# Graph network layer: another order for layernorm's products, and a running-max step or one-hot piece after each max of banks

## The chip, the cores and the metric

The kernel runs on one core of a Trainium2 chip. The metric is device time in microseconds (us), the median of several executions. Engines are named as in the profile: PE (TensorE matmuls; PEld its weight loads), DVE (VectorE), ACT (ScalarE), POOL (GpSimd, which here mostly writes the descriptors of indirect DMAs, "gathers"), SP (SyncE, which issues the plain DMAs).

## The reference, cut to what matters

x is 6250 x 128 (float32); src and dst hold 206250 edges, sorted by dst, with one self loop per node.

```python
h = jnp.maximum(_layernorm(x, axis=-1), 0.0)
x_i, x_j = h[dst], h[src]
feat = jnp.concatenate([x_i, x_j - x_i], axis=-1)
msg = feat @ W.T + b
out = jax.ops.segment_max(msg, dst, num_segments=6250)
return x + jnp.where(jnp.isfinite(out), out, 0.0)
```

Since W is split in two halves, msg is a term of the node itself plus B[src], with B = h @ (second half of W).T. What costs time is the maximum of B's rows over each node's neighbours.

## The kernel before, in words

**First stage (to about 170 us): layernorm, products, and the list of edges.** The 6250 nodes are 125 partitions x 50 columns (Q = 50), worked off two columns at a time. One such step k has three parts. `turn(k)` transposes the normalized rows on PE (L529) and copies them out on ACT (L530). `product(k)` multiplies (L544 the bias row, L547 the weights) into one of two PSUM banks called pm; ACT then makes a rounded copy Bp (L549) and a full copy for the output and for the table Bt in DRAM (L550, tile `acc`, called the stage). `remainder(k)` subtracts the rounded copy from pm on PE (L556), copies what is left to the second half of Bp on ACT (L558), and after each fifth step sends the stage off (SP to Bt, POOL added onto out). The list `micro` holds all of these parts in the order in which they are issued; `ln(n)` issues the next n of them.

Meanwhile DVE and PE work on each partition's window of 1792 edges. DVE compares the list with shifted copies of itself (L636) and PE counts the hits in PSUM (L625, tile `dup`, four banks), until `far()`. Then DVE sums (L743) and packs the list in eleven passes (`pass_(i)`: L672 and L673), and the lists `rest[i]` say what else is issued behind pass i: `spread_0` (PE L754, one transposed column into a pm bank), `spread_a` (DVE L758 to L764 reads that bank; PE L768 follows), `spread_b` (DVE L772 to L777, reads L768's result), `names` (ACT L737 and L738, reads `dup`), `turned` (PE L795 into `dup`, ACT L796 out of it: three tables TD, TV and TQ), and `build(0)`, `build(1)` (DVE L205, L209 and L212: the first one-hot pieces, which need all three tables). From pass 7 on POOL gathers rows of Bt.

**Main loop (to the end): 13 tiles x 25 pairs = 325 pairs.** A pair handles two columns of source nodes for one tile of 490 destinations (392 in the last). PE multiplies Sel by a feature table into z (L990, 2 or 3 matmuls), ACT turns z into a one-hot (L991), PE multiplies Bp's halves by it into `ps` (L1124, 4 or 6 matmuls, one of two double banks), and DVE takes the maximum of both banks into `acc2` (L1133; L1131 for a tile's first). I call this instruction a max of banks. Each reads the acc2 that the one before it wrote, and PE may fill a ps tile again only after the max that read it. At a tile's end L1159 folds acc2.

Between the maxes `fill_in(k)` puts other DVE work: the 395 steps of a running max over gathered rows (L172, `one_row`; each reads the row written by the step before) and the pieces of the one-hots that later tiles need (L205, L209 and L212; `between` is the list of pieces still to do; PE L244 uses them). Each row step k lets POOL issue a gather some rows ahead (L92, X<-Bt; at most 36 ahead), every six steps SP stores six rows to M, and every third step may issue a gather of ends (L92, R<-M). 34 pairs before the end all rows must be done (`more_rows(GR)`); then the last gathers from M (mend, none, R) and the outputs follow.

DVE's order is fixed when the program is built. `fill_in` keeps estimated clocks `tm["pe"]` and `tm["dve"]`, and `due` is the row count that should be reached at pair k. Before, it issues rows while they are more than 5 behind due, then rows up to 12 ahead of due or pieces, as long as DVE's estimated clock lies behind PE's.

Of the kernel before, what the change touches and what calls it, by code (L numbers as in the profile page):

```python
# [36 lines left out]
GR = 396  # L37
# [6 lines left out]
UL = 6  # L44
# [13 lines left out]
def gnn_kernel(tc, x, src, dst, W, b, out):  # L58
# [42 lines left out]
    with ExitStack() as ctx:  # L101
# [14 lines left out]
        with ExitStack() as body:  # L116
# [151 lines left out]
            with ExitStack() as pre:  # L268
# [296 lines left out]
                micro = []  # L565
                for k in range(NP_ + 2):
                    for f, n in ((turn, k), (product, k - 1), (remainder, k - 2)):
                        if 0 <= n < NP_:
                            micro.append((n if f is turn else -1, lambda f=f, n=n: f(n),
                                          {turn: 0.25, product: 1.15, remainder: 0.13}[f]))  # L570
# [151 lines left out]
                dups = s16.bitcast(BF16)  # L722
                ln(18)
                for r in range(2):
# [118 lines left out]
                rest = {i: [] for i in range(12)}  # L843
                rest[0] += [spread_0] + [lambda: ln(6)]
                rest[1] += [lambda: ln(8)]
                rest[2] += [lambda: ln(8), spread_a]
                rest[3] += [lambda: ln(len(micro)), names]
                rest[4] += [spread_b, lambda: turned(TD, (dlc, identb)), lambda: turned(TV, (vm, identb), (low, negL))]
                rest[5] += [clear_early, load_first, lambda: turned(TQ, (dups, sgI), (name, halfI))]
                rest[6] += [lambda: own_last(0), lambda: own_last(1), lambda: own_last(2), lambda: own_last(3)]  # L850
# [50 lines left out]
            with ExitStack() as main:  # L901
# [43 lines left out]
                for p in range(2 * NT):  # L945
                    if p + 2 < len(units):
                        for j, i in enumerate((1, 3, 5) if p % 2 else (2, 5, 8)):
                            n = units[p + 2][1]
                            if 2 * j < n:
                                at_pair(p, i, lambda u_=p + 2, j=j: mats(u_, 2 * j, 2 * j + 2), pe=0.9 + 0.2 * (p % 2 == 0 and j == 0))  # L950
                        if p % 2:
                            for j in range(6):
                                at_pair(p, 5 + j, lambda t=(p + 2) // 2, j=j: feats(t, j), act=0.46 if j < 4 else 0.7)
                    if p + 3 < len(units):
                        at_pair(p, 0, lambda u_=p + 3: (between.extend(zip(pieces(u_), (0.45, 0.45, 0.42, 0.42, 0.48, 0.58) if units[u_][1] == UL
                                                                           else (0.32, 0.32, 0.3, 0.3, 0.35, 0.4))), fill.update(most=6)))
                        for i in range(6, 12):
                            at_pair(p, i, lambda i=i: fill.update(most=11 - i))
# [81 lines left out]
                def fill_in(k):  # L1040
                    due = GR * (k + 1 - wait) / (span_ - wait)
                    until = tm["pe"] + own_pe[k + 1]
                    while len(between) > fill["most"]:
                        one_piece()
                    while state["ran"] < GR:
                        n = state["ran"]
                        if n < due - 5:
                            one_row()
                        elif tm["dve"] + 0.2 > until:
                            break  # L1050
                        elif n < due + 12 and n < state["gathered"] and land[n] <= tm["dve"]:
                            one_row()
                        elif between:
                            one_piece()
                        else:
                            break

# [197 lines left out]
```

## Time and profile before

| what | value |
|---|---|
| runs before | 801.6 us median of 3 (798.94 to 804.96) |
| the profiled execution's own time | 800.41 us |
| its span, first to last instruction | 798.6 us |
| mean granted TensorE clock | 0.964 |

The profile is one execution. Its span is the time from the first to the last instruction; the execution's own time has 1.8 us more around it. The views used are the page (share of each engine), stretches of time (busy time of each engine in each), groups of instructions by form (count, busy time, mean duration), and the timeline, which merges equal neighbouring instructions: "1.51 ... x4" are four instructions that took 1.51 us from the first's start to the last's end. An idle time and what ended it stand in square brackets. On PE a merged row is the only safe measure of speed, because matmuls overlap: the difference between six in a row and four in a row is the cost of two.

### The profile page before, as it was taken

The page shows a single profiled execution, that of the slowest core. Times are in us where ns is not written, and L with a number is a line of the kernel's source. Part 1 is how long each engine was busy: PE and PEld are TensorE (multiplying, and loading weights), DVE is VectorE, ACT ScalarE, POOL GpSimd, SP SyncE. Part 2 cuts the span into 40 slices and gives each one's busy share as a digit, 9 for nine tenths or more (in the row PEclk, how much of TensorE's full clock was granted, in tenths as well). Part 3 has the DMA queues.
Part 4 walks back from the last instruction along what each step waited for, and adds up shares of the span by engine and source line. Part 5 has one row for each costly group of instructions (what it writes and reads, how often), then busy time and mean ns, then how long its engine had stood idle before and what let it go on. Part 6 is the DMA issues. An engine that isn't in the chain of part 4 may idle for free.

```text
span 798.6 us, 12065 instructions
## 1 busy us (share of the span) xinstructions
PE 694.1 (87%) x3776; PEld 513.2 (64%) x3782; DVE 724.7 (91%) x1256; ACT 552.6 (69%) x1162; POOL 476.2 (60%) x519
## 2 busy tenths in 40 slices
PE   0688865668999999999989999999999999999994
PEld 0345544546677667776667767777776677777894
DVE  7999993789899999998999999999999999998885
ACT  4688445365886988879776675866767686776862
POOL 4000012577577777777777777777777777760472
PEclk9999998669999999999999999999999999999997
DMA  6833036133334344343443333434333433341247
GB/s 189 289 66 61 4 67 131 31 81 86 89 84 113 101 112 125 91 109 82 113 105 96 104 92 101 125 90 125 93 102 93 110 93 102 89 120 41 60 81 131
DMA packets 79651, 79.40 MB, mean 99 GB/s; under 512 B 10042, under 2 KB 68495, under 8 KB 79579
## 3 DMA queue, kind: packets, MB, share of 16 engines
q0 software_dynamic: 16560, 37.64, 20.5%
q1 hardware_dynamic: 62667, 40.30, 17.4%
q10 hardware_dynamic: 352, 0.61, 0.3%
q8 instruction: 31, 0.51, 0.3%
q14 instruction: 41, 0.34, 0.1%
HBM read 39.25 MB, written 39.19 MB: 98 GB/s over the span
## 4 chain that ended last, share of the span: by engine, by line
DVE 41%; PE 26%; issue 14%; ACT 12%; DMA 4%; DVEq 0%; POOL 0%; SPq 0%; ACTq 0%; POOLq 0%
DVE acc L1133 18%; PE ps L1124 12%; DVE X L172 8%; ACT oh L991 6%; PE z L990 6%; DVE OHQ L205 3%; PE pv L244 2%; DVE T L636 2%; DMA X<-Bt,ridx 2%; PE pm L547 2%; ACT dump L1163 1%; PE dup L625 1%; DVE dwin L673 1%; ACT Vb L259 1%; PE dup L795 1%
## 5 line engine op out<-in xcount | busy, mean ns | idle before, releaser
L991 ACT ACTIVATE oh<-z 126x490 fp32r<-126x490 f32 (+1 forms) x754 | 381.0, 575 | 157.2 <-PE z L990 154.4
L92 POOL DMA_INDIRECT X<-Bt,ridx x396 | 395.9, 1000 | 134.6 <-issue 38.1
L1124 PE MATMUL ps<-oh,Bp 126*128 126x490 f32 (+1 forms) x1508 | 440.4, 420 | 12.8 <-DVE acc L1133 11.4
L1133 DVE TENSOR_TENSOR acc<-acc,ps 128x980 f32<-128x980 f32 (+1 forms) x312 | 360.4, 1155 | 25.5 <-PE ps L1124 18.2
L1124 PEld LDWEIGHTS ps<-oh,Bp 126*128 126x128 f32 x1508 | 281.1, 192 | 104.1 <-DVE acc L1133 47.9
L990 PE MATMUL z<-Vb,Sel 128*126 128x490 f16 (+1 forms) x650 | 195.8, 373 | 11.3 <-ACT oh L991 6.6
L172 DVE SCALAR_TENSOR_TENSOR X<-X,slim 128x128 f32<-128x128 f32 x395 | 138.8, 351 | 8.4
L990 PEld LDWEIGHTS <-Sel 128*126 128x126 f16 x754 | 99.8, 140 | 46.5 <-issue 12.7
L563 POOL DMA_DIRECT2D out_x<-acc x10 | 9.2, 1129 | 109.2 <-ACT Bp L558 88.3
L244 PEld LDWEIGHTS <-OHQ 128*128 128x128 bf16 x840 | 58.4, 160 | 23.4 <-issue 22.6
L244 PE MATMUL pv<-OHD,OHQ 128*128 128x28 bf16 (+1 forms) x826 | 61.8, 228 | 10.4 <-DVE OHD L212 10.4
L92 POOL DMA_INDIRECT R<-M,last_e x49 | 47.9, 978 | 18.9 <-issue 12.5
L205 DVE TENSOR_TENSOR OHQ<-T,IQ 128x1092 bf16<-128x1092 bf16 (+5 forms) x96 | 57.0, 602 | 0.2 <-DVE badc L898 0.2
L990 PE MATMUL z<-Vf,Sel 128*126 128x490 f16 (+1 forms) x104 | 38.8, 373 | 0.5 <-ACT Vf L259 0.5
L625 PE MATMUL dup<-T,identb 128*128 128x512 bf16 (+1 forms) x159 | 36.0, 358 | 2.0 <-DVE T L636 1.1
L1163 ACT ACTIVATE dump<-lane_dl,nbias 128x472 bf16<-128x472 int32 x50 | 35.2, 704 | 0.1
L547 PE MATMUL pm<-wT,hT 128*125 128x256 f32 x100 | 28.3, 409 | 0.0
L625 PEld LDWEIGHTS <-identb 128*128 128x128 bf16 x164 | 16.2, 99 | 18.7 <-issue 5.0
L544 PE MATMUL pm<-brow,bsel 128*125 128x512 f32 x25 | 13.2, 527 | 16.5 <-ACT Bp L558 14.6
L549 ACT CAST Bp<-pm 125x256 fp32r<-125x256 f32 x25 | 9.3, 371 | 25.6 <-PE pm L547 25.6
L636 DVE TENSOR_TENSOR T<-KA 128x1792 bf16<-128x1792 int16 x20 | 21.3, 1076 | 1.6 <-PE dup L625 1.5
L547 PEld LDWEIGHTS pm<-wT,hT 128*125 128x125 f32 x100 | 20.4, 204 | 3.1
(301 smaller groups left out, 515.8 us busy)
## 6 DMA issues: line engine op xcount, KB each, us to landing
M<-X SPq DMA_DIRECT2D x66, 384.0 KB
X<-Bt,ridx POOLq DMA_INDIRECT x396, 2.6
X<-in_x SPq DMA_DIRECT2D x5, 560.0 KB
out_x<-X SPq DMA_DIRECT2D x5, 560.0 KB
Bt<-acc SPq DMA_DIRECT2D x5, 560.0 KB
out_x<-acc POOLq DMA_DIRECT2D x5, 560.0 KB, 8.7
ownb<-Bt SPq DMA_DIRECT2D x11, 245.0 KB
out_x<-R POOLq DMA_DIRECT2D x5, 480.0 KB, 9.4
```

The source lines that it names most:

```text
L92: i = G_.indirect_dma_start(out=o, out_offset=None, in_=table, in_offset=bass.IndirectOffsetOnAxis(ap=idx, axis=0))
L172: step = V.scalar_tensor_tensor(G[:, j], state["prev"], slim[:, k:k + 1], G[:, j], op0=ALU.min, op1=ALU.max)
L205: return V.tensor_tensor(OHQ[:, :nl, a:z], over(TQ, z - a), iq, ALU.is_equal)
L244: last = T_.matmul(o, w, m, start=False, stop=True, skip_group_check=True)
L547: T_.matmul(pm[:L, j], hT[k % 2][:, j, :L], wT, start=False, stop=j == 1)
L625: T_.matmul(dup[:, a:z], w, e[:, a:z], start=first, stop=last)
L636: V.tensor_tensor(e, KA[:, 64:], i1, ALU.is_equal)
L990: T_.matmul(z[:L + 1, :n], Sel[:, order[i // 2][j]], f[t % 2][:, :n], start=True, stop=True)
L991: A_.activation(oh[:, :n], z[:L + 1, :n], AF.Relu)
L1124: T_.matmul(ps[:, j, :n], w, o[:, :n], start=m == 0, stop=m == len(todo) - 1)
L1133: V.tensor_tensor(a, a, ps[:, :, :n], ALU.max)
L1163: A_.activation(dump, lane_dl, AF.Sign, scale=2.0, bias=nbias[:, c:c + 1], accum_out=ends[:, c:c + 1])
```

## The change

Three things change; no instruction is added or removed.

First, `micro` is ordered turn(k), remainder(k-2), product(k-1) instead of turn(k), product(k-1), remainder(k-2). Second, `ln(30)` instead of `ln(18)` parts are issued right behind `far()`, all the rest of them behind pass 0 (before: in portions behind passes 0 to 3), and `names` and the three `turned` move forward by two or three passes; `spread_0`, `spread_a`, `spread_b`, `clear_early` and `load_first` stay behind their passes. Third, `fill_in` is written anew: after each max it issues at most one row, then alternates a piece and a row while there is reason to, and the assumed costs of pieces are raised.

```diff
-                    for f, n in ((turn, k), (product, k - 1), (remainder, k - 2)):
+                    for f, n in ((turn, k), (remainder, k - 2), (product, k - 1)):
...
-                ln(18)
+                ln(30)
...
-                rest[0] += [spread_0] + [lambda: ln(6)]
-                rest[1] += [lambda: ln(8)]
-                rest[2] += [lambda: ln(8), spread_a]
-                rest[3] += [lambda: ln(len(micro)), names]
-                rest[4] += [spread_b, lambda: turned(TD, (dlc, identb)), lambda: turned(TV, (vm, identb), (low, negL))]
-                rest[5] += [clear_early, load_first, lambda: turned(TQ, (dups, sgI), (name, halfI))]
+                rest[0] += [spread_0, lambda: ln(len(micro)), names]
+                rest[1] += [lambda: turned(TD, (dlc, identb))]
+                rest[2] += [spread_a, lambda: turned(TV, (vm, identb), (low, negL))]
+                rest[3] += [lambda: turned(TQ, (dups, sgI), (name, halfI))]
+                rest[4] += [spread_b]
+                rest[5] += [clear_early, load_first]
...
-                    while len(between) > fill["most"]:
-                        one_piece()
-                    while state["ran"] < GR:
-                        n = state["ran"]
-                        if n < due - 5:
-                            one_row()
-                        elif tm["dve"] + 0.2 > until:
-                            break
-                        elif n < due + 12 and n < state["gathered"] and land[n] <= tm["dve"]:
-                            one_row()
-                        elif between:
-                            one_piece()
-                        else:
-                            break
+
+                    def row():
+                        n = state["ran"]
+                        if n >= GR or not (n < due - 3 or n < due + 8 and n < state["gathered"] and land[n] <= tm["dve"]):
+                            return False
+                        one_row()
+                        return True
+
+                    apart = not row()
+                    while between and (apart or len(between) > fill["most"] or state["ran"] < due - 1 or tm["dve"] + 0.4 < until):
+                        one_piece()
+                        apart = False
+                        if state["ran"] < due + 2 or tm["dve"] + 0.2 < until:
+                            if not row():
+                                break
+                    while state["ran"] < min(due - 4, GR):
+                        one_row()
```

What this does to the engines' order is shown at three places. On PE, in the run of steps behind `far()` (pm is the bank, Bp the rounded copy, pt the transpose; "waits Activation" is a wait for ACT), before:

```order
L544 MATMUL pm_988<-brow_204,bsel_203 125x512 [waits Activation_49]
L547 MATMUL pm_988<-wT_67,hT1_247 125x256 x2
L556 MATMUL pm_976<-Bp_76,negI_243 125x2x128
L529 MATMUL pt_1000<-ident_66,X_79 128x125 [waits PE_49]
L529 MATMUL pt_1000<-ident_66,X_79 128x125
L544 MATMUL pm_1004<-brow_204,bsel_203 125x512 [waits Activation_49]
```

and now:

```order
L544 MATMUL pm_978<-brow_204,bsel_203 125x512 [waits PE_49]
L547 MATMUL pm_978<-wT_67,hT0_246 125x256 x2
L529 MATMUL pt_984<-ident_66,X_79 128x125 [waits PE_49]
L529 MATMUL pt_984<-ident_66,X_79 128x125
L556 MATMUL pm_978<-Bp_76,negI_243 125x2x128 [waits Activation_49]
L544 MATMUL pm_994<-brow_204,bsel_203 125x512 [waits PE_49]
```

Before, the product itself waits for ACT (for L558 of an earlier step, which frees its bank), and the remainder behind it belongs to the step before (pm_976). Now the remainder waits for ACT (for L549 of its own step, pm_978), and the next product follows it without a wait of its own for ACT.

On PE at the end of these steps (L768 is `spread_a`'s, read by `spread_b`; L795 with dlc fills TD, with vm and KB TV), before:

```order
L556 MATMUL pm<-Bp,negI 125x2x128
L768 MATMUL pm<-ones,rows 128x1 x3
L556 MATMUL pm<-Bp,negI 125x2x128
L795 LDWEIGHTS dlc__197
L795 MATMUL dup<-identb,dlc__197 128x128
```

and now:

```order
L795 LDWEIGHTS dlc__197
L795 MATMUL dup<-identb,dlc__197 128x128
L768 MATMUL pm<-ones,rows 128x1 x3
L795 LDWEIGHTS vm
L795 MATMUL dup<-identb,vm 128x128
```

L768 stood ahead of the last remainder and of all tables; now it stands behind the last of TD's fourteen matmuls. L754 (`spread_0`) also moves: six of the fourteen products behind `far()` stood ahead of it, now ten.

On DVE in the main loop's first third (acc2 is the running maximum, ps the banks, X the gathered rows, OHQ and OHD the one-hots), before:

```order
L172 SCALAR_TENSOR_TENSOR X_79<-X_79,slim_90 128x128 x6
L1133 TENSOR_TENSOR acc2_2666<-acc2_2666,ps_3024 128x980
L1133 TENSOR_TENSOR acc2_2666<-acc2_2666,ps_3040 128x980
L172 SCALAR_TENSOR_TENSOR X_79<-X_79,slim_90 128x128 x4
L1133 TENSOR_TENSOR acc2_2666<-acc2_2666,ps_3084 128x980
L172 SCALAR_TENSOR_TENSOR X_79<-X_79,slim_90 128x128 x4
L205 TENSOR_TENSOR OHQ6_1453<-T3_83,IQ_80 128x6x182
L1133 TENSOR_TENSOR acc2_2666<-acc2_2666,ps_3114 128x980
L1133 TENSOR_TENSOR acc2_2666<-acc2_2666,ps_3133 128x980
```

and now:

```order
L1136 TENSOR_TENSOR acc2_2069<-acc2_2069,ps_2577 128x980
L172 SCALAR_TENSOR_TENSOR X_79<-X_79,slim_90 128x128
L1136 TENSOR_TENSOR acc2_2069<-acc2_2069,ps_2598 128x980
L172 SCALAR_TENSOR_TENSOR X_79<-X_79,slim_90 128x128
L209 TENSOR_TENSOR OHD6_1455<-T3_83,IW_81 128x1176
L172 SCALAR_TENSOR_TENSOR X_79<-X_79,slim_90 128x128
L1136 TENSOR_TENSOR acc2_2069<-acc2_2069,ps_2621 128x980
```

Rows came in bunches and maxes one behind the other; now they alternate (the max of banks is line 1136 in the changed file). Counted over the whole loop, a row stands right behind a row 234 times before and never now; a max right behind a max 76 times before and 20 now; the fold L1159 right behind a max 12 times before and 2 now. In the 252 pairs 36 to 287 the three counts are 204, 50 and 10 before, and 0, 0 and 0 now. POOL's own order is the same but for the place of one gather of ends.

More of the change, by code (lines that the diff above doesn't have):

```diff
@@ L954, in gnn_kernel @@
                     if p + 3 < len(units):
-                        at_pair(p, 0, lambda u_=p + 3: (between.extend(zip(pieces(u_), (0.45, 0.45, 0.42, 0.42, 0.48, 0.58) if units[u_][1] == UL
-                                                                           else (0.32, 0.32, 0.3, 0.3, 0.35, 0.4))), fill.update(most=6)))
+                        at_pair(p, 0, lambda u_=p + 3: (between.extend(zip(pieces(u_), (0.62, 0.62, 0.59, 0.59, 0.68, 0.68) if units[u_][1] == UL
+                                                                           else (0.43, 0.43, 0.41, 0.41, 0.48, 0.48))), fill.update(most=6)))
                         for i in range(6, 12):
```

## The prediction

> **What bounds the kernel now.** I read the page's shares first, then the span by stretches, then the timeline at the places that the change touches.
>
> ```profile
> DVE 41%; PE 26%; issue 14%; ACT 12%; DMA 4%; DVEq 0%; POOL 0%; SPq 0%; ACTq 0%; POOLq 0%
> 92.00:134.00 42.00, 26.61 (x121) 20.02 (x120) 26.41 (x32) 21.10 (x57) 5.36 (x7) 0.96 0.34 68
> 134.00:151.00 17.00, 9.23 (x72) 7.85 (x73) 11.66 (x11) 8.97 (x12) 5.17 (x6) 0.51 0.42 86
> 174.00:248.00 74.00, 69.03 (x375) 51.37 (x374) 65.62 (x108) 54.46 (x119) 50.17 (x50) 0.97 0.34 88
> 248.00:464.00 216.00, 201.57 (x1095) 149.77 (x1094) 204.68 (x347) 166.92 (x359) 165.11 (x168) 0.98 0.39 103
> 464.00:734.00 270.00, 260.17 (x1451) 193.93 (x1449) 260.02 (x408) 188.85 (x370) 192.39 (x196) 1.00 0.37 100
> ```
>
> The first row is the page's chain of waits by engine; the others are stretches: length, then busy time (and count) of PE, PEld, DVE, ACT, POOL, then the granted clock, DMA share and GB/s. Two things are to be seen. From 92 to 151 us no engine is full: DVE is busy 38 of 59 us. From 248 to 734 us DVE is busy 464.7 of 486 us and PE 461.7, but a busy PE is not PE at its peak.
>
> How DVE's instructions stand to each other shows what its 486 us are made of (start, length, merged rows):
>
> ```profile
> 404.20 3.73 DVE L1133 TENSOR_TENSOR acc<-acc,ps 128x980 f32<-128x980 f32 x3
> 407.85 1.51 DVE L172 SCALAR_TENSOR_TENSOR X<-X,slim 128x128 f32<-128x128 f32 x4
> 409.27 1.17 DVE L1133 TENSOR_TENSOR acc<-acc,ps 128x980 f32<-128x980 f32 x1
> 411.71 0.33 DVE L172 SCALAR_TENSOR_TENSOR X<-X,slim 128x128 f32<-128x128 f32 x1
> 411.98 1.16 DVE L1133 TENSOR_TENSOR acc<-acc,ps 128x980 f32<-128x980 f32 x1
> ...
> L1133 DVE TENSOR_TENSOR acc<-acc,ps 128x980 f32<-128x980 f32 x243 | 284.4, 1170 | 12.0 <-PE ps L1124 6.0 <-DVE acc L1133 0.5 <-PE z L990 0.5
> L172 DVE SCALAR_TENSOR_TENSOR X<-X,slim 128x128 f32<-128x128 f32 x343 | 120.6, 351 | 7.3
> L1131 DVE TENSOR_TENSOR acc<-ps,acc 128x980 f32<-128x980 f32 x10 | 11.8, 1179 | 1.3
> ```
>
> The last three rows are the groups from 248 to 734 us: 243 + 10 maxes, so 486 / 253 = 1.92 us a pair. Four rows in a bunch take 1.51 us, that is 4 x 0.351 plus three gaps of 0.035. Three maxes take 3.73, that is 3 x 1.17 plus two gaps of 0.11. But the max at 409.27 starts 0.09 us before the rows ahead of it end (407.85 + 1.51 = 409.36), and the one at 411.98 starts 0.06 before the row ahead of it ends; I take 0.084, the median over the loop. An instruction that reads what its predecessor wrote waits for it; one that doesn't overlaps its end.
>
> PE has less to do than its busy time says:
>
> ```profile
> 410.64 1.24 PE L1124 MATMUL ps<-oh,Bp 126*128 126x490 f32 x4
> 412.00 1.69 PE L1124 MATMUL ps<-oh,Bp 126*128 126x490 f32 x6
> 401.22 1.04 PE L244 MATMUL pv<-OHD,OHQ 128*128 128x28 bf16 x14
> 402.10 0.40 PE L990 MATMUL z<-Vf,Sel 128*126 128x490 f16 x1
> 402.34 0.58 PE L990 MATMUL z<-Vb,Sel 128*126 128x490 f16 x2
> ```
>
> Two more ps matmuls cost 0.45 us, 0.225 each; a z 0.18 to 0.21; fourteen pv 1.04, about 0.06 each behind the first. With 1508 ps, 754 z and 840 pv over 325 pairs (the page's counts; z by ACT's 754) PE needs about 4.64 x 0.225 + 2.32 x 0.21 + 0.16 + 0.03 for the rest = 1.72 us a pair. DVE at 1.92 bounds the loop, with PE 10% behind it.
>
> **The change part by part.** First the steps behind far(), PE and ACT rows of one step and the next one's start, then the end of that stage:
>
> ```profile
> 92.48 0.47 PE L544 MATMUL pm<-brow,bsel 128*125 128x512 f32 x1
> ...
> 127.53 0.50 PE L544 MATMUL pm<-brow,bsel 128*125 128x512 f32 x1 [0.89 <-ACT Bp L558]
> 127.87 1.02 PE L547 MATMUL pm<-wT,hT 128*125 128x256 f32 x4
> 128.54 0.47 PE L556 MATMUL pm<-Bp,negI 125*125 125x256 f32 x1
> 130.12 0.50 PE L544 MATMUL pm<-brow,bsel 128*125 128x512 f32 x1 [1.11 <-ACT Bp L558]
> ...
> 128.93 0.37 ACT L549 CAST Bp<-pm 125x256 fp32r<-125x256 f32 x1 [1.17 <-PE pm L547]
> 129.20 0.59 ACT L550 COPY acc<-pm 125x512 f32<-125x512 f32 x1
> 129.67 0.39 ACT L558 CAST Bp<-pm 125x256 fp32r<-125x256 f32 x1
> 133.90 0.37 ACT L558 CAST Bp<-pm 125x256 fp32r<-125x256 f32 x1 [1.24 <-PE pm L556]
> 134.16 1.85 ACT L737 CAST s<-dup 128x512 bf16<-128x512 f32 x4
> ...
> 150.01 0.80 ACT L796 CAST T<-dup 128x768 bf16<-128x768 f32 x1 [1.53 <-PE dup L795]
> ...
> 110.56 0.27 DVE L758 TENSOR_SCALAR rows<-pm 1x128 f32<-1x128 f32 x1
> ...
> 116.87 2.23 DVE L673 COPY_PREDICATED dwin<-big,dwin 128x1776 int32<-128x1776 int32 x1
> 133.58 0.16 DVE L772 CAST cols__105<-pm 128x1 int32<-128x1 f32 x1 [14.49 <-PE pm L768]
> ...
> 134.23 2.12 DVE L672 TENSOR_SCALAR big<-dwin 128x1760 int32<-128x1760 int32 x1
> ...
> 145.57 0.18 DVE L828 TENSOR_SCALAR ridx<-dwin 128x32 int32<-128x32 int32 x1
> 150.85 1.37 DVE L205 TENSOR_TENSOR acc<-T,IQ 128x1092 bf16<-128x1092 bf16 x2 [5.09 <-ACT T L796]
> ```
>
> A step takes 130.12 - 127.53 = 2.59 us: product 1.36, then L549, L550 and L558 on ACT (to 130.06), then the next product. In the new order PE waits only for L549 (129.30), does the remainder (about 0.22 of PE before the next can enter: L556 stands 0.67 behind L547's start, inside its tail) and goes on: 1.40 + 0.37 + 0.05 + 0.22 = 2.04 us. L550, L558 and the next L530 on ACT fit beside it (about 1.4 us of ACT per step). Cover: the transposes L529 lie in the 0.45 us in which PE waits for L549. Fourteen products stood behind far(), from 92.5 to the last L558's end at 134.2. Thirteen intervals save 0.55 each, 7 us; the wait of PE for spread_a's read behind L754 and the low clock after it go too, and the last step's tail, together some 4.5 us. So L737 starts near 122.7 instead of 134.16.
>
> What is late next: L754 now waits behind ten products, to about 113.6, so DVE stands 3 us at L758 behind pass 2 (free at 110.6). L768 now waits for names and TD: its result reaches DVE at 128.7, where DVE, done with passes 3 and 4 near 122.7, has stood 6 us. Then spread_b (0.7) and passes 5 to 7 (134.23 to 145.57, less 1 us by which L672 is longer there than its 1.06 elsewhere) give 139.7; TQ is ready 16.7 us behind L737's start, as before (150.01 + 0.80 - 134.16), at 139.4. build(0) so starts near 139.8 instead of 150.85: **11 us** gained. Bounds: 3 us if the step stays at 2.59 (the other stalls still go), 11.5 if DVE never waits for L768. What follows build(0) keeps its order, so POOL's first gathers and the loop move by the same. SP's and POOL's DMAs of the stage come every 10.2 us instead of 12.9; a stage half is written again 12 us after it was sent, and memset L835's wait for the last one is in the same place; I cost it at nothing, and 1 us more for each group if it doesn't fit.
>
> In the loop each row no longer behind a row gains 0.035 + 0.084 = 0.12 us, each max no longer behind a max 0.105 + 0.084 = 0.19, each fold about 0.12. In pairs 36 to 287 that is 204 x 0.12 + 50 x 0.19 + 10 x 0.12 = 35 us of DVE, 0.14 a pair: its own need (464.7 us busy and some 13 us of such gaps) falls from 1.90 to 1.76. PE's 1.72 is now only 2% below, and in a pair the one or the other has more (PE 1.3 with four ps, 2.0 with six; DVE 1.35 with a row, 2.1 with a piece between two rows). The two ps tiles let DVE lag by one pair, so I take neighbouring pairs two by two, PE's one pair ahead, and the larger of both sums: for the order of before that gives 1.927 us a pair, where 1.92 was measured; for the new one 1.850. Bounds: 1.79 (DVE's need and the 0.03 a pair that stand over it now), 1.895 (each pair alone). 252 x 0.077 gives **19 us** (26 to 8). Pairs 0 to 35 (the stretch from 174 to 248 us) have 0.12 a pair less on DVE too, but a colder PE there: **2 us** (0 to 4). The last 37 pairs have no rows: nothing.
>
> [...]
>
> Then POOL, a floor under all of it:
>
> ```profile
> 501.15 0.94 POOL L92 DMA_INDIRECT X<-Bt,ridx  x1 [0.30 <-issue]
> 502.40 0.94 POOL L92 DMA_INDIRECT X<-Bt,ridx  x1 [0.30 <-DVE X L172]
> ...
> L92 POOL DMA_INDIRECT X<-Bt,ridx x396: 940/944/3984, 146.0 to 711.1; - x198
> L172 DVE SCALAR_TENSOR_TENSOR X<-X,slim x395: 333/352/417, 181.1 to 739.9; 128x128 f32<-128x128 f32 x198
> ```
>
> From 248 us POOL issues a gather every 216 / 168 = 1.29 us with nothing but its own 0.30 us between: it is full, and its last gather at 711.1 leads the last row at 739.9 by 29 us. If its gathers only move with the first stage, the last comes near 700, lands some 3 us later, and the rows can't end before 703, 37 us earlier than now. The sum is 11 + 2 + 19 = **32 us**, so this floor isn't reached, but of the lead only some 8 us are left. The profiled execution took 800.41 us and would take 768; the median before is 1.2 us above that execution.
>
> **The rivals.** (1) The gathers take the bound: if POOL's start doesn't move by 11 us (it waits for row steps early on) or its mean interval grows, the rows wait for landings. With the last gather where it is, rows end at 714, 26 us earlier: 774; with intervals 1.5% longer as well (390 x 1.29 x 0.015 = 7.5 us), up to 782. For it: POOL has no slack. Against it: nothing of its own order changes. (2) DVE's order is worth nothing: only the first stage gains, 789. The overlaps above speak against it. [...] (3) PE and DVE interlock better than two by two: 1.79 a pair, a gain of 46 by DVE alone, cut by POOL's floor at 37 and a few us more if its early gathers gain too: 757 to 763. (4) Slower: they interlock worse, in lockstep. If the row and piece behind each max hold the bank so long that PE's next pair starts only when that is over, each pair costs the larger of both with no lag: 2.015 us by the same durations. That is 252 x 0.09 + 3 = 26 us lost and 11 gained: 815. It is slower than before once a pair costs over 1.97. Against it: the same reckoning for before gives 2.15, where 1.92 was measured.
>
> **How the numbers follow.** Forecast (the sum, 762 to 774) 0.62; rival 1 (774 to 782) 0.15; rival 3 (755 to 762) 0.14; rival 2 (785 to 793) 0.06; rival 4 0.03. Some 0.85 of this lies between 754 and 782. One per cent is 8 us, about what a measurement can tell from no change; all cases but the upper end of rival 2 and rival 4 are faster by more: faster 0.94, within 1% 0.03, slower 0.03.
>
> **What would show it.** Steps behind far() at 2.04 us; DVE idle twice, 3 us ahead of L758 and 6 ahead of L772; build(0) near 140. In the loop, rows of one each with starts before their predecessor's end, DVE's busy share under 95%, about 1.85 us a pair, and PE's weight loads waiting less for DVE; the last gather near 700 and the last row within 10 us of it. DVE waiting at L172 for landed gathers shows rival 1; rows that start at their predecessor's end, rival 2; PE idle in each pair before ps, rival 4. The prediction is wrong if the overlap belongs to chance and not to dependence, or if the loop's pace stays at 1.92.

## The result, and the profile after

| what | before | changed |
|---|---|---|
| median of 4 runs, us | 800.27 (796.66 to 804.96) | 779.61 (778.53 to 781.03) |
| profiled execution's own time, and its span | 800.41, 798.6 | 781.03, 779.3 |

The ratio is 0.974, with a 95% interval from 0.968 to 0.980: 20.7 us faster where 32 were forecast. Ten of the twelve runs further down met chips on which the kernel before took 1065 to 1079 us instead of 800; those are read by their ratio to the kernel before on the same chip, and by their traces. The ratios leave out runs over 1.5% above the fastest of the same kernel, so they can differ a little from the ratio of the medians.

First the chain of waits by engine, then stretches as in the prediction (length, busy time and count of PE, PEld, DVE, ACT, POOL, clock, DMA share, GB/s). They are cut at the maxes of banks that start pairs 0, 36, 252 and 288; the file has three lines more, so the max is L1136 and ps L1127.

```profile
PE 43%; DVE 20%; ACT 17%; issue 10%; DMA 7%; POOL 2%; SPq 0%; DVEq 0%; POOLq 0%; ACTq 0%
166.00:237.00 71.00, 66.03 (x371) 50.77 (x370) 63.56 (x108) 53.30 (x116) 54.16 (x56) 0.98 0.35 97
237.00:642.00 405.00, 386.01 (x2160) 296.59 (x2159) 384.96 (x649) 310.09 (x640) 312.05 (x306) 1.00 0.37 104
642.00:716.00 74.00, 69.27 (x389) 53.30 (x388) 63.65 (x109) 46.89 (x92) 56.97 (x56) 0.95 0.34 97
```

The same two last stretches of the kernel before:

```profile
248.00:667.00 419.00, 396.31 (x2161) 293.59 (x2159) 401.06 (x651) 309.56 (x638) 320.26 (x325) 0.99 0.39 104
667.00:734.00 67.00, 65.44 (x385) 50.11 (x384) 63.65 (x104) 46.22 (x91) 37.23 (x39) 1.00 0.32 88
```

DVE led the chain with 41%; now PE does with 43%. In pairs 36 to 251 DVE is busy 16.1 us less and the stretch is 14 us shorter. In pairs 252 to 287 DVE has the same 63.65 us of work, but needs 74 us for it instead of 67. The table gives each stretch's length to a tenth, by the maxes' starts and the end of the span, and what the prediction's terms had for it (its 0.077 a pair over 216 and 36 pairs).

| stretch | before | changed | gain | forecast |
|---|---|---|---|---|
| to the first max | 173.7 | 165.7 | 8.0 | 11 |
| pairs 0 to 35 | 74.0 | 71.3 | 2.7 | 2 |
| pairs 36 to 251 | 419.4 | 405.5 | 13.9 | 16.6 |
| pairs 252 to 287 | 66.8 | 73.2 | -6.4 | 2.8 |
| pair 288 to the end | 64.7 | 63.6 | 1.1 | 0 |

The first stage's places, in the order of their times (start, length, what ended the idle time before): two remainders with ACT's copies between them, DVE's two stands, the first one-hot piece, POOL's first gathers.

```profile
94.66 0.38 PE L556 MATMUL pm<-Bp,negI 125*125 125x256 f32 x1 [0.73 <-ACT acc L550]
...
96.17 0.37 ACT L549 CAST Bp<-pm 125x256 fp32r<-125x256 f32 x1 [0.72 <-PE pm L547]
96.44 0.59 ACT L550 COPY acc<-pm 125x512 f32<-125x512 f32 x1
...
97.09 0.39 PE L556 MATMUL pm<-Bp,negI 125*125 125x256 f32 x1 [0.73 <-ACT acc L550]
...
114.83 0.28 DVE L758 TENSOR_SCALAR rows<-pm 1x128 f32<-1x128 f32 x1 [7.41 <-PE pm L754]
131.83 0.16 DVE L772 CAST cols__105<-pm 128x1 int32<-128x1 f32 x1 [8.45 <-PE pm L768]
142.41 0.18 DVE L828 TENSOR_SCALAR ridx<-dwin 128x32 int32<-128x32 int32 x1
142.81 0.73 DVE L205 TENSOR_TENSOR acc<-T,IQ 128x1092 bf16<-128x1092 bf16 x1 [0.22 <-issue]
...
142.87 1.62 POOL L92 DMA_INDIRECT X<-Bt,ridx  x1 [7.88 <-DVE ridx L828]
...
148.14 4.69 POOL L92 DMA_INDIRECT X<-Bt,ridx  x1 [0.30 <-issue]
```

A step takes 97.09 - 94.66 = 2.43 us, not 2.04: the remainder starts when L550 has ended, not L549. build(0) is 8.0 us earlier (142.81 against 150.85), the first gather only 3.2 (142.87; before 146.03).

In the loop, DVE's instructions from the timeline:

```profile
400.68 0.34 DVE L172 SCALAR_TENSOR_TENSOR X<-X,slim 128x128 f32<-128x128 f32 x1
400.99 1.18 DVE L1136 TENSOR_TENSOR acc<-acc,ps 128x980 f32<-128x980 f32 x1
402.08 0.39 DVE L172 SCALAR_TENSOR_TENSOR X<-X,slim 128x128 f32<-128x128 f32 x1
402.39 0.67 DVE L205 TENSOR_TENSOR OHQ<-T,IQ 128x1008 bf16<-128x1008 bf16 x1
402.98 0.34 DVE L172 SCALAR_TENSOR_TENSOR X<-X,slim 128x128 f32<-128x128 f32 x1
```

Each starts 0.03 to 0.09 us before its predecessor ends (402.08 + 0.39 = 402.47, and the piece starts at 402.39). The page's groups of POOL's gathers, of the max and of PE's weight loads ahead of ps (count, busy time and mean ns, idle time before them and what ended most of it), in the changed kernel:

```profile
L92 POOL DMA_INDIRECT X<-Bt,ridx x396 | 409.6, 1034 | 128.3 <-issue 37.8
...
L1136 DVE TENSOR_TENSOR acc<-acc,ps 128x980 f32<-128x980 f32 (+1 forms) x312 | 360.1, 1154 | 39.9 <-PE ps L1127 35.5
L1127 PEld LDWEIGHTS ps<-oh,Bp 126*128 126x128 f32 x1508 | 286.0, 192 | 87.0 <-DVE acc L1136 19.2
```

and on the page of the kernel before:

```profile
L92 POOL DMA_INDIRECT X<-Bt,ridx x396 | 395.9, 1000 | 134.6 <-issue 38.1
...
L1133 DVE TENSOR_TENSOR acc<-acc,ps 128x980 f32<-128x980 f32 (+1 forms) x312 | 360.4, 1155 | 25.5 <-PE ps L1124 18.2
L1124 PEld LDWEIGHTS ps<-oh,Bp 126*128 126x128 f32 x1508 | 281.1, 192 | 104.1 <-DVE acc L1133 47.9
```

Ahead of ps PE's weight loads wait 28.7 us less for DVE (all their idle time is 17.1 us less), but DVE's maxes wait 17.3 us more for PE.

Last, all gathers of X and all rows by their lines (count, shortest, median and longest ns, first and last start):

```profile
L92 POOL DMA_INDIRECT X<-Bt,ridx x396: 940/945/4692, 142.9 to 711.0; - x198
L172 DVE SCALAR_TENSOR_TENSOR X<-X,slim x395: 333/344/407, 168.7 to 718.2; 128x128 f32<-128x128 f32 x198
```

and from the timeline the longest stand of a row and the gather that it waited for:

```profile
678.19 1.72 POOL L92 DMA_INDIRECT X<-Bt,ridx  x1 [0.30 <-DVE acc L1136]
...
682.82 0.35 DVE L172 SCALAR_TENSOR_TENSOR X<-X,slim 128x128 f32<-128x128 f32 x1 [2.37 <-issue]
```

The last gather starts at 711.0, as before (711.1), and the last row follows 7 us behind it, where it was 29. The row at 682.82 has caught up with the gather issued at 678.19.

### The profile page after: what moved, and what is told of

Its sections match the earlier page's. It is cut to its first block, busy times and chain, and to the rows that moved or that the text cites. A ratio compares the mean times of both kernels' runs of the same rounds, so it can differ in the third digit from the quotient of the medians.

```text
span 779.3 us, 12126 instructions
## 1 busy us (share of the span) xinstructions
PE 684.6 (88%) x3776; PEld 517.3 (66%) x3782; DVE 703.4 (90%) x1256; ACT 553.7 (71%) x1162; POOL 489.7 (63%) x519
## 4 chain that ended last, share of the span: by engine, by line
PE 43%; DVE 20%; ACT 17%; issue 10%; DMA 7%; POOL 2%; SPq 0%; DVEq 0%; POOLq 0%; ACTq 0%
PE ps L1127 22%; PE z L990 10%; ACT oh L991 9%; DVE acc L1136 6%; PE pv L244 6%; DMA X<-Bt,ridx 5%; DVE T L636 3%; DVE X L172 3%; ACT Vb L259 2%; PE pm L547 1%; ACT Vf L259 1%; ACT dump L1166 1%; DVE dwin L673 1%; ACT acc L550 1%; POOL X L92 1%
## 5 line engine op out<-in xcount | busy, mean ns | idle before, releaser
L92 POOL DMA_INDIRECT X<-Bt,ridx x396 | 409.6, 1034 | 128.3 <-issue 37.8
L1127 PE MATMUL ps<-oh,Bp 126*128 126x490 f32 (+1 forms) x1508 | 445.4, 423 | 10.0 <-DVE acc L1136 9.7
L1136 DVE TENSOR_TENSOR acc<-acc,ps 128x980 f32<-128x980 f32 (+1 forms) x312 | 360.1, 1154 | 39.9 <-PE ps L1127 35.5
L1127 PEld LDWEIGHTS ps<-oh,Bp 126*128 126x128 f32 x1508 | 286.0, 192 | 87.0 <-DVE acc L1136 19.2
L990 PE MATMUL z<-Vb,Sel 128*126 128x490 f16 (+1 forms) x650 | 198.0, 373 | 13.8 <-ACT oh L991 7.7
L172 DVE SCALAR_TENSOR_TENSOR X<-X,slim 128x128 f32<-128x128 f32 x395 | 136.1, 345 | 4.0 <-issue 2.4
L205 DVE TENSOR_TENSOR OHQ<-T,IQ 128x1092 bf16<-128x1092 bf16 (+5 forms) x96 | 57.4, 601 | 0.2 <-DVE badc L898 0.2
L625 PEld LDWEIGHTS <-identb 128*128 128x128 bf16 x164 | 16.1, 99 | 19.2 <-issue 5.1
L547 PE MATMUL pm<-wT,hT 128*125 128x256 f32 x100 | 26.5, 388 | 0.0
L673 DVE COPY_PREDICATED dwin<-big,dwin 128x472 int32<-128x472 int32 (+10 forms) x12 | 21.9, 1826 | 0.4
L549 ACT CAST Bp<-pm 125x256 fp32r<-125x256 f32 x25 | 9.3, 371 | 18.0 <-PE pm L547 17.8
L636 DVE TENSOR_TENSOR T<-KA,KB 128x1792 bf16<-128x1792 int16 x21 | 21.1, 1081 | 0.0
L547 PEld LDWEIGHTS pm<-wT,hT 128*125 128x125 f32 x100 | 19.3, 193 | 2.7
```

The lines of the kernel that those rows point to most:

```text
L92: i = G_.indirect_dma_start(out=o, out_offset=None, in_=table, in_offset=bass.IndirectOffsetOnAxis(ap=idx, axis=0))
L172: step = V.scalar_tensor_tensor(G[:, j], state["prev"], slim[:, k:k + 1], G[:, j], op0=ALU.min, op1=ALU.max)
L205: return V.tensor_tensor(OHQ[:, :nl, a:z], over(TQ, z - a), iq, ALU.is_equal)
L547: T_.matmul(pm[:L, j], hT[k % 2][:, j, :L], wT, start=False, stop=j == 1)
L625: T_.matmul(dup[:, a:z], w, e[:, a:z], start=first, stop=last)
L636: V.tensor_tensor(e, KA[:, 64:], i1, ALU.is_equal)
```

## The experiments

Theory 1 was: POOL's gathers, which start only 3.2 us earlier, end where they ended, and so cap the loop. The rival: PE, ACT and DVE set the pace, and gathers don't matter.

**e1: the first stage's part alone; e2 and e6: the loop's part alone** (the same kernel twice). e1 is the kernel before with

```diff
-                    for f, n in ((turn, k), (product, k - 1), (remainder, k - 2)):
+                    for f, n in ((turn, k), (remainder, k - 2), (product, k - 1)):
...
-                ln(18)
+                ln(30)
```

and the new lists `rest`; e2 and e6 have the new `fill_in` and the new costs of pieces instead.

> The first stage's part of the change alone, on the loop of before. The first max of banks should start about 8 us earlier than before (165.7 against 173.7), and the loop's order stays. Theory 1 (in the changed kernel POOL's gathers cap the end of the rows, in the kernel before they do not, since its rows lag the gathers by 24 us or more): all 8 us reach the end, 800.3 - 8.0 = 792.3. Rival (rows already stand on the gathers in the loop of before, whose first gather moves by 3.2 us only): 797.

> The loop's part alone (fill_in and the costs of the pieces), with the first stage of before. First gather back at 146.0 (142.9 in the changed kernel), first max back at 173.7 (165.7). Theory 1 (the chain of gathers caps the end): only the gathers' start counts, 779.6 + 3.2 = 782.8. Rival (pace of the pairs alone, the two parts add up): 779.6 + 8.0 = 787.6.

> The kernel of e2 again, for the same reason: the loop's part alone. Theory 1 (the gathers' start counts, 3.2 us later than in the changed kernel): 782.8, ratio 0.978. Rival (the first stage's 8.0 us are lost in full): 787.6, ratio 0.984. If the chip is one at about 1067, ratio 0.904 as in e2.

Measured: e1 1065.5 us, ratio 0.997 (0.992 to 1.002); e2 962.2, 0.904 (0.899 to 0.910); e6 961.9, 0.899 (0.892 to 0.906). On these chips the loop's part makes the kernel 10% faster and the first stage's next to nothing; neither theory's number can be read from them, since no row waits for a gather there (the last row starts 48 to 56 us behind the last gather, and no row less than 28 us behind the end of its own). The traces give the first stage apart from the loop: with its part alone, steps of 2.43 us; without it, 2.59 in e6, and in e2 2.59 at first and 3.72 from 111 us on, where the granted clock was 0.50.

**e8: the changed kernel on these chips.** No edit.

> The changed kernel itself, unchanged, on the chips of the experiments. e3, e4, e5 and e7 can be read only against it: if it takes about 955 too, neither the ends gathered late, nor the earlier first gathers, nor the split copy moved the end here. If gathers capped the end on these chips as well (theory 1), it should take 5 us or more above e4 (952.2), that is 957 or more, with the last rows within 10 us of their gathers; if rows lag by 50 us here, as in e1 to e4, it should lie within 3 us of e4.

Measured: 965.2 us (955.2 to 971.2), ratio 0.9065 (0.899 to 0.914). The last row starts 46 us behind the last gather, so gathers cap nothing there. It lies 13 us above e4 where at most 3 were expected, but on another chip, and its own four runs are 16 us apart.

**e3 and e5: ends of lists gathered behind all of X** (the same kernel twice).

```diff
-                    if state["ran"] % 3 == 0:
-                        get_rows(1)
```

> The changed kernel with one line less: the ends of the lists are no longer gathered one behind every third row among the gathers of X, but all behind the last row. POOL then has some 30 gathers (about 39 us of POOL at 1.3 us each) less to do before the last gather of X. Theory 1: the last gather of X ends near 675 instead of 711, rows never wait for a landing, pairs 252 to 288 fall from 2.035 to about 1.85 us, so 779.6 - 6.7 = 773; the gathers of ends then run beside the last pairs. Rival (the pace at the end is set by PE and DVE, not by gathers): 779.6, within 1.

> The kernel of e3 again: on the chip of e1 to e4 the kernel before took 1067.8 us instead of 800.3, engines stood for several us at a time without work in hand, and the rows lagged the gathers by 50 us or more, so that a cap by gathers could not show. On a chip where the kernel before takes about 800: theory 1 (the chain of gathers caps the end) says ratio 0.966 (773), last gather of X near 675, pairs 252 to 288 at 1.85 us; the rival (PE and DVE set the pace at the end) says 0.974 (779.6). If the chip is again one at about 1067, ratio 0.894 as in e3, and nothing is told apart.

Measured: 955.1 us, ratio 0.894 (0.886 to 0.901), and 955.8, 0.887 (0.880 to 0.895). Of the cap this tells nothing, but it shows what is different on these chips. Stretch of e3 with the 32 gathers of ends in a row, and the max that stands in it:

```profile
784.00:832.00 48.00, 8.05 (x37) 5.46 (x36) 7.23 (x12) 4.20 (x8) 30.80 (x33) 0.61 0.18 46
...
822.30 1.17 DVE L1136 TENSOR_TENSOR acc<-acc,ps 128x980 f32<-128x980 f32 x1 [32.04 <-remote]
```

While POOL issues gathers without a pause, PE, DVE and ACT are busy 8, 7 and 4 of 48 us. By pair 252 e3 was ahead of e8 (759 against 804 us), and it lost that here (875 against 876 us at pair 288).

**e4: first gathers ahead of DVE's stands.** Against the changed kernel:

```diff
-                rest[0] += [spread_0, lambda: ln(len(micro)), names]
+                rest[0] += [lambda: ln(len(micro)), names, spread_0]
...
-                rest[2] += [spread_a, lambda: turned(TV, (vm, identb), (low, negL))]
-                rest[3] += [lambda: turned(TQ, (dups, sgI), (name, halfI))]
-                rest[4] += [spread_b]
-                rest[5] += [clear_early, load_first]
+                rest[2] += [lambda: turned(TV, (vm, identb), (low, negL))]
+                rest[5] += [clear_early, load_first, spread_a, lambda: turned(TQ, (dups, sgI), (name, halfI))]
...
-                rest[7] += [begin_rows, lambda: build(0)]
+                rest[7] += [begin_rows, spread_b, lambda: own_last(0), lambda: own_last(1), lambda: own_last(2), lambda: own_last(3),
+                            lambda: build(0)]
```

> The changed kernel with the first stage's spread sums placed so that VectorE does not stand 7.4 and 8.5 us ahead of pass 7: their TensorE products go behind the last remainder and behind the turned TV, and the first gathers ahead of the wait for the second. First gather at 135.2 (as soon as POOL has cleared its columns) instead of 142.9, first max of banks near 165.7 as before. Theory 1: the chain of gathers ends 7.7 us earlier, the last 36 pairs run at 1.85 instead of 2.035 us, 779.6 - 6.7 = 773. Rival (pace of the pairs): 779.6, within 1.

Measured: 952.2 us, ratio 0.893 (0.887 to 0.898). DVE in e4:

```profile
133.95 0.18 DVE L828 TENSOR_SCALAR ridx<-dwin 128x32 int32<-128x32 int32 x1
137.25 0.16 DVE L772 CAST cols__105<-pm 128x1 int32<-128x1 f32 x1 [3.12 <-PE pm L768]
142.46 2.55 DVE L205 TENSOR_TENSOR acc<-T,IQ 128x1092 bf16<-128x1092 bf16 x4 [4.48 <-ACT T L796]
```

The first gather starts at 135.10, as expected, and pass 7 ends 8.5 us earlier, but build(0) only 0.35 us earlier: it then waits for TQ. So the stands cost the gathers their start and the loop next to nothing.

**e7: ACT's full copy in two halves.**

```diff
-                    A_.copy(stage[:, g, :, o:o + 2].rearrange("l b q c -> l q b c"),
-                            pm[:L].rearrange("l q (b c) -> l q b c", b=2))
+                    for h in range(2):
+                        A_.copy(stage[:, g, h, o:o + 2], pm[:L, :, h * C:h * C + C])
```

> The changed kernel with ScalarE's full copy of a product (L550, 0.59 us, both halves) split into a copy of the first half and one of the second (about 0.37 us each), so that the remainder, which writes the first half, has to wait for the first copy alone. If L550 is what keeps the first stage's step at 2.43 us instead of 2.04: the wait of L556 of 0.73 us falls to about 0.5, the step comes down to 2.1 to 2.3 us, and the transposing copies after the last remainder (L737, at 125.2) start 2 to 5 us earlier. If the step is bound by something else (ScalarE's own 1.72 us a step, which grows to 1.87): the step stays at 2.43 or grows by 0.15. Of the total, under theory 1 (first gathers wait behind VectorE's two stands, which end with TensorE's list): a gain of 2 to 5 us; if the stands stay, none.

Measured: 956.8 us, ratio 0.900 (0.890 to 0.910); steps of 2.49 us. In e7 the remainder's row is

```profile
95.51 0.38 PE L556 MATMUL pm<-Bp,negI 125*125 125x256 f32 x1 [0.80 <-ACT acc L551]
```

and L551 x2 runs from 94.81 to 95.46: it still waits for both halves, though it writes the first alone. In this step only the second of the two copies updates the semaphore (a counter that one instruction raises and another waits for) that L556 waits for, so the wait for both is written into the program, and the split did not do what it was meant to do. The step follows the end of ACT's last copy out of the bank (it grew by 0.06 us as that did), but how short it is without that wait was not measured.

**e9: builds behind passes 8 to 10.** e4, with

```diff
-                            lambda: build(0)]
...
-                rest[8] += [lambda: build(1), first_own] + [lambda j=j: feats(0, j) for j in range(6)]
...
+                for f in [lambda: build(0), lambda: build(1), first_own] + [lambda j=j: feats(0, j) for j in range(6)]:
+                    f()
```

the last two lines behind the block of small sums.

> e4, and besides the builds of the first two units, the first transposes of the own rows and the first features go behind passes 8 to 10 and the block of small sums (L861 to L898), so that VectorE works through its wait of 4.5 us for the last turned copy. First gathers in a row from 135.1 on (20 of them, not 3 and then a wait for the builds), first max of banks at 156 to 161 instead of 165.7 to 167. If the loop's own pace sets the end: 5 to 9 us less than e4, about 944. If gathers cap it: less by the gathers' start alone, 952 (nothing). If the 20 gathers in a row hold the other engines up, as 34 gathers of list ends in a row did in e3 and e5 (VectorE stood 32 us there): first max at 167 or later, and no gain.

Measured: 952.6 us, ratio 0.892 (0.883 to 0.900); the changed kernel on the same chip (e8) had 0.9065. The third branch came true: 18 gathers in a row, to 166.5, and PE, DVE and ACT nearly still until 168.

```profile
160.00:168.00 8.00, 1.63 (x8) 0.86 (x7) 0.00 (x0) 0.00 (x0) 4.98 (x6) 0.50 0.20 51
```

The first max came near 176. The total is that of e4 all the same.

**e10 and e11: both kernels without the loop's gathers.** Both met a chip on which the kernel before takes 799.4 us.

```diff
-                    gather(ring(k // U)[:, k % U], Bt[:, :], ridx[:, k:k + 1], behind)
+                    if k < GB * U: gather(ring(k // U)[:, k % U], Bt[:, :], ridx[:, k:k + 1], behind)
```

> The changed kernel without the gathers of X behind the first 42 (one filling of the ring): rows then run on what the ring holds, so the output is another; TensorE's, ScalarE's and VectorE's instructions are the same, the 49 gathers of list ends stay. Theory 1 (on the chip of the first profile gathers cap the last 36 pairs at 2.035 us instead of about 1.85, and cost nothing else): 779.6 - 6.7 = 773. Rival (pace of PE, ACT and DVE alone): 779.6. On the chips of e1 to e9, where the changed kernel takes 965: if gathers are what holds the engines there, the time falls by some 185 us to these 773 to 780; if it is the chip or its clock, it stays within 20 us of 965.

> The kernel before with the same left out (gathers of X behind the first 42; other output). Its rows lagged their gathers by 24 us or more on the chip of the first profile, so nothing should be gained there: 800, within 3, and the loop's and first stage's parts of the change together are then worth 27 us without gathers against 20.7 with them (theory 1), or 20.7 both times (rival). On the chips of e1 to e9, where the kernel before takes 1066: about 800 if gathers hold the engines, within 20 us of 1066 if not.

Measured: e10 778.6 us (777.6 to 780.3), ratio 0.971 (0.961 to 0.980); e11 803.0, 1.000 (0.994 to 1.006). The totals decide nothing: the interval of e10 holds both the 773 of theory 1 (0.967) and the rival's 779.6 (0.975), and the ratios of e10 and e11 differ by 24 us, where theory 1 had 27 and the rival 20.7. The stretches say more. Pairs 36 to 251 and 252 to 287 of e10:

```profile
239.00:644.00 405.00, 386.22 (x2161) 296.87 (x2160) 384.40 (x648) 310.27 (x640) 28.78 (x28) 1.00 0.21 59
644.00:712.00 68.00, 65.31 (x388) 51.36 (x387) 63.49 (x108) 46.52 (x92) 4.54 (x4) 1.00 0.19 54
```

and of e11:

```profile
251.00:671.00 420.00, 397.47 (x2163) 294.91 (x2162) 400.91 (x653) 310.27 (x639) 26.91 (x28) 0.99 0.20 57
671.00:737.00 66.00, 64.43 (x380) 49.44 (x379) 63.13 (x102) 45.98 (x91) 3.84 (x4) 1.00 0.18 51
```

In 216 pairs nothing changes: 405 us with 306 gathers and with 28 (those of ends alone). In pairs 252 to 287 the same 63.5 us of DVE's work take 68 us instead of 74 (67.6 and 73.2 to a tenth): there gathers cost 5.6 us, near the 6.7 of theory 1, and in the kernel before nothing (66.8 us with them, 66.7 without). Of that 4.0 reach the last outputs, and then the end takes most of it back. The issue of the last outputs on SP's queue, in e10 and then in the changed kernel:

```profile
769.60 0.34 SPq L1181 DMA_DIRECT2D out_x<-ownb  x1
```

```profile
773.60 0.34 SPq L1181 DMA_DIRECT2D out_x<-ownb  x1
```

The closing drains of POOL's queue (shortest, median and longest ns, first and last start), again e10 first:

```profile
L1254 POOLq DRAIN  x3: 46/107/11659, 766.0 to 778.2; - x3
```

```profile
L1254 POOLq DRAIN  x3: 50/107/6744, 770.4 to 779.1; - x3
```

POOL's long drain ends at 766.0 + 11.66 = 777.7 in e10, and all engines wait for it; in the changed kernel at 777.1, before the others are done. Why it takes 5 us longer behind fewer gathers was not tried; in e11 it takes 10.5 us and there, too, ends last. Without it e10 would have ended some 3 us earlier, near 776.

**e12: both remedies.** e4 and e3 together, with build(0), build(1), the first transposes and features in `rest[9]`, so behind passes 8 and 9.

> The changed kernel with two remedies: the list ends gathered behind all gathers of X (e3), and the spread sums late as in e4, with passes 8 and 9 ahead of the builds of the first two units, in VectorE's wait of 4.5 us for the last turned copy. Two prices: the cap by gathers, 3.9 us (the maxes of pair 288 at 711.8 in e10 against 715.7 in the changed kernel), and a first max 4.4 us earlier (161.3 instead of 165.7). If both are on the path on a chip where the kernel before takes 800: 779.6 - 3.9 - 4.4 = 771, ratio 0.965. If only the gathers were (the loop gives the earlier start back while it waits for the first features): 775.7, ratio 0.970. If neither: 779.6, 0.974. On a chip where the kernel before takes 1066, where gathers in a row hold TensorE: 945 to 955, and nothing is told of the two.

Measured: 974.6 us, where 945 to 955 were expected, ratio 0.897 (0.891 to 0.902), on a chip at 1079: the first max came at 179.2, later than in the changed kernel, and there was again a stand with the gathers of ends in a row. It tells nothing of a chip at 800. So no version was shown to beat the changed kernel there.

## Why the prediction was partly off

The direction held, and the mechanisms of the two main terms did; the terms were mis-sized. The 779.6 us lie in the stretch of times that rival 1 had (774 to 782, chance 0.15), not in the forecast's own (762 to 774), but rival 1 came true in part only: its cap by gathers explains 5.6 of the 13 us by which the traces' gain (19.3) stays below 32. That the time fell into rival 1's stretch is luck, since the other losses were none of its own.

Two sums of the prediction do not come out. The upper bound of 26 us for the loop does not follow from 1.79 us a pair, which gives (1.927 - 1.79) x 252 = 35. The chances for 755 to 782 add up to 0.91, where it has "some 0.85".

**The first stage, 11 forecast, 8.0 measured.** The step that failed is "In the new order PE waits only for L549". It waits for L550 as well (0.73 us in each step), because L550 still reads the half that the remainder overwrites; in the steps shown L549 updates no semaphore, and L550 updates the one that L556 waits for. The step is 2.43 us, not 2.04. So L737 starts at 125.2 instead of 122.7, TQ is ready at 142.3 instead of 139.4, and build(0) follows at 142.8 instead of 139.8. The stands at L758 and L772 were told in the right places but at 3 and 6 us instead of 7.4 and 8.5 (DVE was free for the first at 107.4, not at 110.6); e4 shows that this costs build(0) only 0.35 us.

**"POOL's first gathers and the loop move by the same".** The loop moved by 8.0, the gathers by 3.2. The rows for it were there: before, L828 ran at 145.57, 5 us ahead of build(0), because DVE waited for TQ behind it; now pass 7 and TQ come together. Where gathers start is set by pass 7, and there the two long stands count (e4: 135.1 without them).

**The loop, 19 forecast, 7.5 measured (13.9 - 6.4).** That dependence and not chance makes the gaps is borne out: neighbours that don't depend on each other overlap in every row shown, and DVE's busy time fell by 16.1 us in 216 pairs. Nor is it that like stands behind like: in the loop of the kernel before seven pieces of L205 stand right behind another one, on which they don't depend, and start 0.08 us (median) before its end. In the trace each of the 234 rows behind a row waits for a semaphore that the row ahead updates, so the gap is a wait written into the program. Two things were mis-sized.

First the interlock. Taking pairs two by two gave 1.850 us a pair; 405.5 / 216 = 1.877 was measured, and e10 has 1.876 without gathers, so POOL has no part in it. DVE's waits for ps grew from 18.2 to 35.5 us: what DVE saves, it partly spends on waiting for PE. That alone would leave the gain 5.8 us below the forecast; since the kernel before ran at 1.942 there and not at the 1.927 of the same reckoning, it is 2.7 us below, and this offset is luck. What a finer order would win back was not tried.

Then the last 36 pairs. The forecast spread one mean over all 252; there the kernel before already ran at 66.8 / 36 = 1.86, and without gathers the changed one runs at 1.88 (e10): nothing to gain. Of the 204 rows that stood behind a row only 18 stood there, of the 50 maxes behind a max 8, and the changed kernel has 50 rows in these pairs where the kernel before has 45. On top of it comes rival 1, which had 0.15: the last gather did not move (711.0), and the rows caught up with it. That costs 5.6 us: rows stood 4.0 us for gathers, and the granted clock of the stretch is 0.95, where it is 1.00 in e10; how the rest divides was not tried. The floor of 700 for the last gather was too low by 11 us: 7.8 by the start that moved too little, and 3.1 because the chain from the first gather to the last takes 568.2 us instead of 565.1. A gather of X now takes 1034 ns in the mean instead of 1000, which is 13.7 us in all; the rest of it was made up by shorter idle times between them.

The other rivals: DVE's order is not worth nothing: in the rows from 400.68 on, as in those before, a next instruction starts 0.03 to 0.09 us before its predecessor's end. The Trainium skill's page "VectorE: DVE Perf Modes", section "The DRAIN you can't avoid", has the next operation start only when the pipe is empty, but adds that one that is not held starts earlier; these rows agree with the addition. Lockstep (2.015) and the better interlock (1.79) did not come.

## What to carry to other kernels

A remainder placed right behind its product, on an engine whose order is fixed, made the next product wait for every copy out of that bank here, not just for the one whose result it needs; count all the readers, and see which of them the program's semaphores wait for. When several streams feed one loop, ask for each what its own first step waits for: a stage that ends 8 us earlier can move one stream by 8 and another by 3, and the slower one is met again at the far end of the loop. And where order is made better on the bounding engine, expect part of it back as waiting for the next one, and look at each stretch of the loop by itself instead of taking one mean.

## What the runs showed that was not expected

On the four chips of e1 to e9 and e12, the other engines stand while gathers are issued in a row: PE, DVE and ACT do 8, 7 and 4 us of work in 48 us in e3, 1.6, 0 and 0 in 8 us in e9. On the chip of the first profile PE is busy throughout under the same load, with eight gathers in this stretch and 0.30 us between them:

```profile
171.00:180.00 9.00, 9.00 (x63) 7.22 (x62) 8.35 (x15) 5.37 (x12) 6.80 (x8) 1.00 0.34 95
```

Where the time goes can be seen in the changed kernel on such a chip (e8). ACT's one-hots, first on the first chip and then in e8:

```profile
L991 ACT ACTIVATE oh<-z 126x490 fp32r<-126x490 f32 (+1 forms) x754 | 380.9, 575 | 146.4 <-PE z L990 143.5
```

```profile
L991 ACT ACTIVATE oh<-z 126x490 fp32r<-126x490 f32 (+1 forms) x754 | 384.1, 575 | 314.4 <-PE z L990 156.2
```

The work is the same, but ACT is idle 168 us longer ahead of it, nearly all of the 174 us by which the span grew. In 49 of the 754 cases in e8 the one-hot starts over 1 us (up to 11.2, together 153 us) after the recorded end of the z that it reads, though ACT is free; on the first chip there is no such case. The maxes are late in the same way: 49 in e8, none on the first chip, and in e3 the one at 822.30 reads banks that PE had filled at 786.95. So what comes late is the next engine's start, not the work.

What holds the engines is open; e10 and e11, which leave the gathers out, met a chip without it. That gathers are the cause is not shown: in e8 POOL is at a gather in 61% of those 153 us, and in 56% of the whole loop. Loading of instructions does not explain e3's stand: its queues moved no instructions from 776 to 832 us, and ACT went on at 806. The order of before lets gathers follow its rows in bunches, the new one lets them come singly, which would fit the 10% that the loop's part is worth there (e2, e6) against less than 2% on the first chip; the late one-hots add up to 222 us with the old order of the loop (e1) and 154 with the new one (e2). Why the order matters to them was argued, not tried.

A gather's descriptors also take longer beside some of VectorE's work: the one at 148.14 took 4.69 us instead of 0.94. VectorE in that time:

```profile
147.75 2.08 DVE L673 COPY_PREDICATED dwin<-big,dwin 128x1536 int32<-128x1536 int32 x1
149.72 1.81 DVE L205 TENSOR_TENSOR acc<-T,IQ 128x728 bf16<-128x728 bf16 x4
151.45 0.56 DVE L209 TENSOR_TENSOR acc<-T,IW 128x784 bf16<-128x784 bf16 x1
152.04 0.57 DVE L212 TENSOR_TENSOR acc<-acc,T 128x784 bf16<-128x784 bf16 x1
```

The gather ends at 152.83, 0.2 us behind the last of them. The Trainium skill's page "SBUF — State Buffer", section "SBUF: two separate sides", has it that VectorE in some modes holds a port that GpSimd needs to write descriptors, until the instruction ends; this row agrees, though in which mode these instructions ran the trace does not say. In the loop, where pieces stand alone among rows and maxes, the longest gather behind 170 us took 1.72 us.
